# GpSimd in the order of the text from the first step on, a tile's ten gathers spread over the parts of a slot, each behind a ScalarE instruction

## The chip, the cores and the metric

The kernel runs on one core of one Trainium2 chip. The metric is device time in microseconds, the median of several runs. Profile times are microseconds from the start of the profiled execution's span. Engines: PE is TensorE's matmul part, PEld its weight loads, DVE VectorE, ACT ScalarE, POOL GpSimd, SP SyncE (which issues most DMAs, and shows as SPq). L889 is line 889 of the kernel before.

## The reference

A graph layer on N = 3327 nodes with D = 256 features. The input x is (3327, 256), adj is (3327, 3327), a sparse matrix with some 0.12% of its entries and the diagonal set.

```python
h = jnp.maximum(_layernorm(x), 0.0)
R = adj + I;  R = R / R.sum(-1, keepdims=True)
Z = 0;  Xf = h;  Xa = h
for n in range(2):
    A = _top_p_attention(Xa, W1, W2, W3)   # softmax of (Xa W1' W2')(Xa W3')',
    Xf = R @ Xf                            # cut to the top 0.9 of each row's mass, renormalised
    Xa = A @ Xa
    Z = Z + Xf @ U1[n].T + Xa @ U2[n].T
out = x + layernorm(h + Z) * ln_g + ln_b
```

## The kernel before

`guess_graph_layer` (L344) holds the run. The nodes are cut into NT = 26 tiles of 128 rows. Each of the two steps is a loop of slots, `for i in range(-1, NT + 2)`. In slot i tile i's softmax row (128 x 3328) gets its threshold and is scaled (VectorE L726, L731 to L764, L760; `settle`), the logits of tile i + 1 are made (TensorE L598, ScalarE L602 to L608; `measured`), and tile i − 1's row is turned by TensorE in blocks of four (L806), copied by ScalarE (L808) and summed with the nodes (L820; `Sums`). Queries and keys of later tiles come from L521 to L543 (`project`): a TensorE product L521, ScalarE copies L526 and L530, VectorE L536, and five small GpSimd instructions L539 to L543; GpSimd's L641 to L644 are four more small ones, for ScalarE's L652.

The sparse product R @ Xf is done by gathers. `listed` loads the adjacency of a tile in pieces of 256 KB (L841, tag `at`, two buffers, issued by SyncE), reduces each on VectorE (L842), and finds which 128-column blocks of each row hold an entry. The first four block numbers of a row go to `index[:, t, :4]` (GpSimd L851); the rest is packed by TensorE and ScalarE (`packed`, then L874 to L878) and VectorE's L881 into a fifth (GpSimd L882). With these a tile has ten gathers, indirect DMAs that GpSimd issues: five 128 x 128 pieces of the adjacency into `ac` (L889), five of node rows into `xg` (L898, 257 wide, from the table `bx`). A sixth block of `ac`, the diagonal one, comes by SyncE (L884) and gets the identity added by GpSimd (L886). Both tags have two buffers. Two slots later `spread` (L1075 on) multiplies them on TensorE (`diffuse`, L906), stores `ac` for the second step (`cx`, L1084, 384 KB, by SyncE, which waits until all six blocks are there), and writes the result on VectorE (L1087, L1088). `products` makes the tables `ax` and `bx` from the nodes at the start (L987, L993 and the stores L994, L995), through buffers that also hold the exponentials of L602. `first_end` (L914 on) has GpSimd's L923.

The order of work is written by hand. A slot has 7 parts; `PLAN` (L1104), with `BEGIN` for the first slots, is a string of letters for each part, and each letter moves one generator to its next `yield`: m measured, d settle, s spread, w weights, q project, e first_end, a the lister, p packed, g gathers, b products. A generator that is not through at the end of the slot is run to its end. After the letters of a part come the turns (L806, L808) and sums (L820). At the end (L1191 on), the instructions of TensorE, ScalarE and VectorE are chained in the text's order from `begin` on; those of GpSimd only from `ordered[0]` on, which is the start of the second step. In the first step GpSimd's order, and SyncE's throughout, is left to the scheduler. Most slots of the first step have this order on GpSimd: one xg, four ac, one xg, L886, two xg, L923, L882, the fifth ac, the fifth xg, L539 to L543, L641 to L644. On SyncE a slot has 5 or 6 loads L841, with sx (L924), cx (L1084), L884, own (L1078), vx (L1090) and s1 between them.

Of the kernel before, what the change touches and what calls it, by code (L numbers as in the profile page):

```python
# [14 lines left out]
ALU = mybir.AluOpType  # L15
# [5 lines left out]
D = 256  # L21
DA = 64
NT = (N + P - 1) // P
# [312 lines left out]
DIRECT = 4  # L336
LIST = 16
KT = DIRECT + 2
IN_ORDER = mybir.DependencyInfo(mybir.DependencyClass.NoSync, mybir.DependencyReason.DATA)
NONE = NP - 1  # L340

# [2 lines left out]
def guess_graph_layer(ctx, tc, x, adj, w1t, w2t, w3t, u1t, u2t, ln_g, ln_b, out, flag):  # L344
# [15 lines left out]
    V, G, S, PE = nc.vector, nc.gpsimd, nc.scalar, nc.tensor  # L360

    rows_of = lambda t: min(P, N - t * P)
    valid = lambda t: 0 <= t < NT
# [22 lines left out]
    ident = const.tile([P, P], F32, tag="ident", name="ident")  # L386
# [24 lines left out]
    one = const.tile([P, 8], F32, tag="one", name="one")  # L411
# [28 lines left out]
    bx = dram.tile([P, NT, D + 1], F32, tag="bx", name="bx")  # L440
# [429 lines left out]
    def gathered(t):  # L870
        oh = ohs.pop(t)
        ls, n = lists[:, t, :], LIST - DIRECT
        po = ps_t.tile([P, 4, P], F32, tag="pt", name="po")
        PE.matmul(po[:, 0, : n + 1], oh, ls[:, DIRECT:], start=True, stop=True)  # L874
        lo = small.tile([P, n], F32, tag="lo", name="lo", bufs=2)
        S.copy(lo, po[:, 0, :n])
        nth = small.tile([P, 1], F32, tag="nth", name="nth")
        S.activation(nth, po[:, 0, n : n + 1], AF.Identity, scale=-1.0, bias=part)  # L878
        yield
        of = small.tile([P, LIST], F32, tag="of", name="of", bufs=2)  # L880
        V.scalar_tensor_tensor(of[:, :n], place[:, :n], nth, lo, ALU.is_equal, ALU.mult, accum_out=nth)  # L881
        G.tensor_scalar(index[:, t, DIRECT:], nth, -1.0, float(NONE), ALU.mult, ALU.add)  # L882
        ac = adjp.tile([P, KT, P], F32, tag="ac", name="ac", bufs=2)
        nc.sync.dma_start(ac[:, KT - 1, :], adj[t, :, t, :])  # L884
        acs[t] = ac
        G.tensor_tensor(ac[:, KT - 1, :], ac[:, KT - 1, :], ident, ALU.add)  # L886
        rows = adj.rearrange("t p j r -> (t p j) r")
        for k in range(KT - 1):
            G.indirect_dma_start(out=ac[:, k, :], out_offset=None, in_=rows,  # L889
                                 in_offset=bass.IndirectOffsetOnAxis(ap=index[:, t, k : k + 1], axis=0),  # L890
                                 element_offset=t * P * NT * P)
        run(fetched(bx, t, D + 1))

    def fetched(table, t, w):
        xgs[t] = xg = adjp.tile([P, KT - 1, D + 1], F32, tag="xg", name="xg", bufs=2)
        rows = table.rearrange("p j d -> (p j) d")
        for k in range(KT - 1):
            G.indirect_dma_start(out=xg[:, k, :w], out_offset=None, in_=rows,  # L898
                                 in_offset=bass.IndirectOffsetOnAxis(ap=index[:, t, k : k + 1], axis=0))
            yield  # L900
# [59 lines left out]
    none = iter(())  # L960

    def run(work, n=99):
        for _ in range(n):
            next(work, None)
# [40 lines left out]
    for q in range(HALF + 5):  # L1005
        if 0 <= q - 3 < HALF:
            k, pk = q - 3, made.pop(q - 3)
# [86 lines left out]
    def refetch(t):  # L1094
        acs[t] = adjp.tile([P, KT, P], F32, tag="ac", name="ac", bufs=2)
        nc.sync.dma_start(acs[t].rearrange("p k r -> p (k r)"), cx[t])
        yield from fetched(vx, t, D)
# [3 lines left out]

    PLAN = (("mdsssa", "mcdsssa", "edawwp", "msda", "mpdea", "gdawwq", "emgq"),  # L1104
            ("llcmss", "lnms", "lwwnfd", "lcmdsssggggg", "fsmwqdf", "llmdf", "lmwd"))

    LAST = {NT - 1: ("cfss", "cn", "nd", "sss", "fdddddsf", "f", ""), NT: ("c", "", "", "ff", "ff", "fv", "f"),
            NT + 1: ("fv", "f", "", "", "f", "f", "f")}
    BEGIN = {-1: ("mba", "mmbba", "mwwbbaa", "bmwwb", "", "", ""),
             0: ("mdbba", "mcdbba", "medbwwbap", "mdabb", "mpdbwwba", "gdabbq", "q"),  # L1110
             1: ("mdsssbba", "mcdsssbba", "edbawwbp", "msdbga", "mpdea", "dawwq", "emgq")}
    OPEN = {-1: ("llcmss", "lnms", "lwwnfd", "lcmdsssggggg", "fmgswqdf", "llmdf", "lmwfdm"),
            0: ("cmssggg", "nms", "wwnfd", "cmdsss", "fsmgwqdf", "mdf", "mwd"),
            1: ("cmss", "nms", "wwnfd", "cmdsssggggg", "fsmwqdf", "mgdf", "mwd")}
    OPEN[2] = OPEN[3] = OPEN[1]
    fetching = itertools.chain(*(refetch(t) for t in range(NT)))
    LATE = (1, 4)
    BLOCKS = ({}, {1: (0, 1), 2: ()})
# [3 lines left out]
    ordered = []  # L1122
    for step in range(2):
        sums = Sums(step, live, xw if step else x0, AHEAD[step])

        for i in range(-1, NT + 2):
            if step == 0 and i == NT - 3:
                begun = [weights(1, t, live, False) for t in range(3)]
            if step == 1 and i == -1:
                ordered.append(len(trace))  # L1130
            if step == 1 and i == -1:
                run(begun[0])
                prove(0)
                for e in es[4:]:
                    G.memset(e[:, N:NP], 0.0)
            work.update(
                n=work["m"],
                c=work["d"],
                d=settle(step, i, live[step, i]) if valid(i) else none,
                m=measured(step, live[step, i + 1]) if valid(i + 1) else none,  # L1140
                s=spread(step, i - 2 + 2 * step) if valid(i - 2 + 2 * step) else none,
                w=later.pop((step, i + 2), none),
                e=first_end(i - 2) if step == 0 and valid(i - 2) else none,
                a=itertools.islice(lister, 5 + i % 2 if i > 0 else 6) if step == 0 else none,
                p=packed(i + 1) if step == 0 and i >= 0 and valid(i + 1) else none,
                g=fetching if step else itertools.chain(work.get("g", none), gathered(i)) if valid(i) else none,
                b=none if step else product, q=none, v=proof() if step and i == NT else work.get("v", none),
                l=laws(range(3, NT)) if step and i == -1 else work["l"] if step and i == 0 else none,
            )
            if i >= 0 and valid(i + 3):  # L1150
                later[step, i + 3] = weights(step, i + 3, live)
                work["q"] = itertools.islice(later[step, i + 3], 2 - step)
            if step == 0 and i >= NT - 2 and i < NT + 1:

                work["w"] = itertools.islice(begun[i - NT + 2], CUT - 1)
            if step == 0 and i >= NT - 3 and i < NT:
                work["q"] = itertools.islice(begun[i - NT + 3], 1)
            if i == -1:
                work["w"] = begun[1] if step == 0 else itertools.chain(begun[1], begun[2])
            if step == 0 and i == 0:  # L1160
                work["w"] = begun[2]
            for k in range(PARTS):
                g = PARTS * (i - 1) + k - LATE[step]
                summing = valid(g // PARTS)
                if step and valid((g + AHEAD[1]) // PARTS):
                    sums.turn(g + (k == 2), min(i, NT - 1))
                for c in ({**OPEN, **LAST} if step else BEGIN).get(i, PLAN[step])[k]:
                    next(work[c], None)
                if summing and not step:
                    sums.turn(g, min(i, NT - 1))  # L1170
                for n in BLOCKS[step].get(k, (0,)) if summing else ():
                    ended = sums.sum(g + n)
                    if ended and step == 0:
                        live["r", ended[0]] = ended[1]
                    elif ended:
                        work["f"] = finish(ended[0], live.pop(("f", ended[0])), *ended[1])
            if step == 1 and i == -1:
                run(work["m"])
            if step == 0 and i == -1:
                G.memset(es[2][:, N:NP], 0.0)  # L1180
            if step and i < 1:
                next(fetching)
            for c in ("lcnwqsepb" if i > -1 else "cnwqsepb") if step else "cmwqsep" + "gb" * (i > 0):
                run(work[c])
            if step == 0 and i == NT:
                moments(1, gsum)
                for t in range(3):
                    live[1, t]["ms"] = returned(project(1, t, queries=False))
    run(work["f"])

    for engine, since in ((PE.engine, begin), (S.engine, begin), (V.engine, begin), (G.engine, ordered[0])):  # L1191
        queue = [i for i in trace[since:] if i.engine == engine]
        for one_, next_ in zip(queue, queue[1:]):
            tc.add_manual_dep(next_, one_.name, IN_ORDER, reason="order of the text")

# [43 lines left out]
```

## Time and profile before

| what | value |
|---|---|
| median of 3 runs | 1396.95 us (1394.01 to 1402.68) |
| profiled execution | 1402.92 us, span 1401.2 us, clock 0.98 |
| busy: PE, PEld | 1276.6 us (91%), 976.5 us (70%) |
| busy: DVE, ACT, POOL | 1199.8 us (86%), 1102.5 us (79%), 814.9 us (58%) |
| gathers from in_adj, L889 | 130, 142.8 us busy, 1099 ns each |
| gathers from bx, L898 | 130, 165.0 us busy, 1269 ns each |
| SyncE at L1084 waiting for ac | 112.1 us, 25 times |
| first step, by the stretches used | start to 130 us, 130 to 710 us |

The page has a busy time for each engine and, in its fifth part, groups of instructions by line: busy time, mean duration, then the idle time just ahead of them on their engine and what ended it. The waits list, for each line, what ended a wait, the total, how often and the longest. The timeline gives single instructions: start, duration, engine, line, output and inputs, and in brackets the idle time before it with what ended it. For a gather, the duration on POOL is the work of issuing it.

### The profile page before, as it was taken

What the parts mean: (1) busy time and instruction counts of PE and PEld (TensorE: products, weight loads), DVE (VectorE), ACT (ScalarE), POOL (GpSimd) and SP (SyncE); (2) the same over time, 40 slices, a digit from 0 to 9 for tenths busy, and PEclk for the clock granted to TensorE, in tenths of its full rate; (3) what the DMA queues carried; (4) which work ended last, traced back from release to release, by engine and by line L of the source; (5) the groups of instructions that cost most, each with busy time, mean ns of one, the idle gap of its engine ahead of it and who ended that gap; (6) DMA issues with size and microseconds to landing.
All of it is one profiled execution on the core that took longest, in us unless ns stands there. A gap on an engine that the chain in (4) does not pass through costs nothing.

```text
span 1401.2 us, 22108 instructions
## 1 busy us (share of the span) xinstructions
PE 1276.6 (91%) x6495; PEld 976.5 (70%) x6495; DVE 1199.8 (86%) x3689; ACT 1102.5 (79%) x2445; POOL 814.9 (58%) x1244
## 2 busy tenths in 40 slices
PE   5898899999999999999999769999999999999985
PEld 4535777777777777677677547777777777777764
DVE  6878788989999899889882589999998999999984
ACT  5566686778887788778764689999999999999941
POOL 6213888766777667566573475655645556555522
PEclk9999999999999999999999879999999999999998
DMA  8754454453444545444432221221322213122200
GB/s 290 242 167 141 126 153 132 124 148 111 140 142 127 140 117 151 124 126 134 114 82 79 62 63 53 79 84 53 91 61 75 79 58 91 57 79 80 57 20 22
DMA packets 92642, 149.77 MB, mean 107 GB/s; under 512 B 15425, under 2 KB 59072, under 8 KB 92512
## 3 DMA queue, kind: packets, MB, share of 16 engines
q1 hardware_dynamic: 75056, 105.37, 23.9%
q0 software_dynamic: 16640, 42.69, 12.3%
q8 instruction: 54, 0.88, 0.3%
q14 instruction: 76, 0.62, 0.1%
q10 hardware_dynamic: 816, 0.20, 0.1%
HBM read 120.93 MB, written 27.28 MB: 106 GB/s over the span
## 4 chain that ended last, share of the span: by engine, by line
DVE 43%; PE 41%; ACT 9%; issue 5%; POOL 1%; DMA 1%; SPq 0%; DVEq 0%; POOLq 0%; ACTq 0%
PE pa L820 17%; DVE cand L731 9%; DVE w L726 8%; PE pt L806 5%; DVE e L760 5%; PE pl L598 4%; PE pr L906 4%; DVE cand L740 4%; DVE bb L738 3%; PE pz L919 3%; ACT ja L631 3%; DVE x L760 2%; PE pz L987 2%; ACT eT L808 1%; DVE fm L842 1%
## 5 line engine op out<-in xcount | busy, mean ns | idle before, releaser
L820 PE MATMUL pa<-xw,eT 128*128 128x256 f32 x1352 | 324.8, 385 | 27.4 <-DVE s L930 26.2
L631 ACT ACTIVATE ja<-e,g 128x3328 uint8<-128x3328 f32 x106 | 325.8, 3073 | 0.1
L820 PE MATMUL pa<-x,eT 128*128 128x256 f32 x1352 | 324.1, 381 | 0.0
L820 PEld LDWEIGHTS pa<-xw,eT 128*128 128x128 f32 x1352 | 251.6, 191 | 78.2 <-DVE s L930 31.6
L808 ACT COPY eT<-pt 128x512 f32<-128x512 f32 (+1 forms) x364 | 200.7, 559 | 106.5 <-PE pt L806 76.1
L820 PEld LDWEIGHTS pa<-x,eT 128*128 128x128 f32 x1352 | 244.3, 191 | 26.1
L731 DVE MAX8 cand<-w 128x8 f32<-128x168 f32 (+1 forms) x1040 | 251.4, 317 | 0.0
L898 POOL DMA_INDIRECT xg<-bx,index x130 | 165.0, 1269 | 52.0 <-issue 41.6
L806 PE MATMUL pt<-ident,e 128*128 128x128 f32 x1144 | 176.5, 277 | 15.2 <-DVE e L757 9.1
L806 PEld LDWEIGHTS pt<-ident,e 128*128 128x128 f32 x1144 | 141.0, 144 | 55.2 <-issue 27.9
L889 POOL DMA_INDIRECT ac<-in_adj,index x130 | 142.8, 1099 | 43.9 <-issue 29.1
L726 DVE SCALAR_TENSOR_TENSOR w<-e,g 128x3328 f32<-128x3328 f32 x44 | 162.1, 3684 | 0.7
L898 POOL DMA_INDIRECT xg<-vx,index x130 | 129.5, 996 | 38.6 <-issue 38.6
L906 PE MATMUL pr<-xg,ac 128*128 128x257 f32 (+1 forms) x520 | 141.9, 397 | 9.9 <-DVE s L1088 6.3
L760 DVE SCALAR_TENSOR_TENSOR e<-e,rec 128x3328 f32<-128x3328 f32 x40 | 147.7, 3691 | 0.6
L602 ACT ACTIVATE e<-pl 128x832 f32<-128x832 f32 x132 | 113.7, 866 | 16.4 <-PE pl L598 12.0
L906 PEld LDWEIGHTS pr<-xg,ac 128*128 128x128 f32 x520 | 94.2, 195 | 36.4 <-issue 14.6
L738 DVE MAX8 bb<-cand 128x8 f32<-128x160 f32 x286 | 92.6, 324 | 6.7 <-DVE cand L740 0.3
L598 PE MATMUL pl<-both,qT 64*128 64x416 f32 x416 | 91.7, 542 | 6.5 <-DVE e L993 3.5
L598 PE MATMUL pl<-after,qT 64*128 64x416 f32 x416 | 95.9, 555 | 0.0
L842 DVE TENSOR_REDUCE fm<-at 128x4 f32<-128x512 f32 (+1 forms) x133 | 84.5, 635 | 12.8 <-DMA at<-in_adj 11.8
L674 POOL TENSOR_SCALAR g<-g,law 128x1 f32<-128x1 f32 x23 | 46.4, 2016 | 67.1 <-ACT g L673 67.1
(258 smaller groups left out, 2087.3 us busy)
## 6 DMA issues: line engine op xcount, KB each, us to landing
at<-in_adj SPq DMA_DIRECT2D x114, 256.0 KB
cx<-ac SPq DMA_DIRECT2D x26, 384.0 KB
ac<-cx SPq DMA_DIRECT2D x26, 384.0 KB
wide<-in_adj SPq DMA_DIRECT2D x8, 832.0 KB
e<-in_adj SPq DMA_DIRECT2D x6, 832.0 KB
own<-bx SPq DMA_DIRECT2D x26, 128.5 KB
x<-in_x SPq DMA_DIRECT2D x13, 256.0 KB
s<-ax SPq DMA_DIRECT2D x26, 128.0 KB
```

The costliest lines, as they stand in the source:

```text
L598: PE.matmul(pl[:, a, :wd], qT[p, :], keys_of(step, a).rearrange("p a b -> p (a b)")[:, c : c + wd], start=True, stop=True)
L631: S.activation(ja, e, f, bias=guess, scale=sign, accum_out=total)
L726: V.scalar_tensor_tensor(w, e, col(16), e, ALU.is_lt, ALU.mult, accum_out=d2)
L731: V.max(cand[:, 8 * s : 8 * s + 8], w[:, s * SEG : min(NP, (s + 1) * SEG)])
L738: V.max(b8, cand)
L760: V.scalar_tensor_tensor(e, e, at(1), e, ALU.is_ge, ALU.mult, accum_out=ra)
L806: PE.transpose(pt[:, j, :], e[:, (j0 + j) * P : (j0 + j + 1) * P], ident)
L808: S.copy(eT[:, :w, :], pt[:, :w, :])
L820: PE.matmul(self.pa, eT[:, c - 4 * k, :], self.xa[:, j, :], start=c == 0, stop=c == NT - 1)
L889: G.indirect_dma_start(out=ac[:, k, :], out_offset=None, in_=rows, in_offset=bass.IndirectOffsetOnAxis(ap=index[:, t, k : k + 1], axis=0), ...
L898: G.indirect_dma_start(out=xg[:, k, :w], out_offset=None, in_=rows, in_offset=bass.IndirectOffsetOnAxis(ap=index[:, t, k : k + 1], axis=0))
L906: PE.matmul(pr[:, :w], ac[:, k, :], own if k == KT - 1 else xg[:, k, :w], start=k == 0, stop=k == KT - 1)
```

## The change

GpSimd is chained in the text's order from `begin` on. `gathered` is split in two. Its first half (new letter h) makes the fifth block number. The gathers are a chain of their own, `spacing`, in which each letter g issues one. `spaced` gives the order for a tile: ac 0 to 3, xg 0 to 3, the fifth ac with the identity addition, the fifth xg; for tiles 0 and 1 together: five ac of tile 0, four of tile 1, five xg of tile 0, the fifth ac of tile 1, five xg of tile 1. `PLAN` has ten g in a slot, one or two in a part. The first GpSimd instruction of each g gets a dependence (`BEHIND`) on the last ScalarE instruction that stands ahead of it in the text. (The fifth pair of a tile is issued at the start of the slot after.) The diff, cut to its core:

```diff
--- before.py
+++ after.py
@@ -336,6 +336,7 @@
 DIRECT = 4
 LIST = 16
 KT = DIRECT + 2
+BEHIND = mybir.DependencyInfo(mybir.DependencyClass.Sync, mybir.DependencyReason.DATA)
 IN_ORDER = mybir.DependencyInfo(mybir.DependencyClass.NoSync, mybir.DependencyReason.DATA)
 NONE = NP - 1
 
@@ -880,16 +881,27 @@
         of = small.tile([P, LIST], F32, tag="of", name="of", bufs=2)
         V.scalar_tensor_tensor(of[:, :n], place[:, :n], nth, lo, ALU.is_equal, ALU.mult, accum_out=nth)
         G.tensor_scalar(index[:, t, DIRECT:], nth, -1.0, float(NONE), ALU.mult, ALU.add)
+
+    def adjacent(t):
         ac = adjp.tile([P, KT, P], F32, tag="ac", name="ac", bufs=2)
         nc.sync.dma_start(ac[:, KT - 1, :], adj[t, :, t, :])
         acs[t] = ac
-        G.tensor_tensor(ac[:, KT - 1, :], ac[:, KT - 1, :], ident, ALU.add)
         rows = adj.rearrange("t p j r -> (t p j) r")
         for k in range(KT - 1):
             G.indirect_dma_start(out=ac[:, k, :], out_offset=None, in_=rows,
                                  in_offset=bass.IndirectOffsetOnAxis(ap=index[:, t, k : k + 1], axis=0),
                                  element_offset=t * P * NT * P)
-        run(fetched(bx, t, D + 1))
+            if k == KT - 2:
+                G.tensor_tensor(ac[:, KT - 1, :], ac[:, KT - 1, :], ident, ALU.add)
+            yield
+
+    def spaced(few):
+
+        both_ = [(adjacent(t), fetched(bx, t, D + 1)) for t in few]
+        if len(few) > 1:
+            (a, f), (b, h) = both_
+            return itertools.chain(a, itertools.islice(b, DIRECT), f, b, h)
+        return itertools.chain(*(itertools.islice(a, n) for n in (DIRECT, 1) for a in both_[0]))
 
     def fetched(table, t, w):
         xgs[t] = xg = adjp.tile([P, KT - 1, D + 1], F32, tag="xg", name="xg", bufs=2)
@@ -1101,18 +1113,20 @@
 
 
 
-    PLAN = (("mdsssa", "mcdsssa", "edawwp", "msda", "mpdea", "gdawwq", "emgq"),
+    PLAN = (("gmdsssa", "gmcdsssa", "edawwpg", "gmsdga", "gmpdea", "hgdawwqg", "gehmgq"),
             ("llcmss", "lnms", "lwwnfd", "lcmdsssggggg", "fsmwqdf", "llmdf", "lmwd"))
 
     LAST = {NT - 1: ("cfss", "cn", "nd", "sss", "fdddddsf", "f", ""), NT: ("c", "", "", "ff", "ff", "fv", "f"),
             NT + 1: ("fv", "f", "", "", "f", "f", "f")}
     BEGIN = {-1: ("mba", "mmbba", "mwwbbaa", "bmwwb", "", "", ""),
-             0: ("mdbba", "mcdbba", "medbwwbap", "mdabb", "mpdbwwba", "gdabbq", "q"),
-             1: ("mdsssbba", "mcdsssbba", "edbawwbp", "msdbga", "mpdea", "dawwq", "emgq")}
+             0: ("mdbba", "mcdbba", "medbwwbap", "mdabb", "gmpdbwwba", "hgdabgbq", "hgq"),
+             1: ("ggmdsssbba", "gmcdgsssbba", "gedbawwbp", "msdbga", "gmpdeag", "hgdawwqg", "hgemgq"),
+             2: ("gmdsssa", "gmcdsssga", "gedawwpg", "gmsdga", "gmpdea", "hgdawwqg", "gehmgq")}
     OPEN = {-1: ("llcmss", "lnms", "lwwnfd", "lcmdsssggggg", "fmgswqdf", "llmdf", "lmwfdm"),
             0: ("cmssggg", "nms", "wwnfd", "cmdsss", "fsmgwqdf", "mdf", "mwd"),
             1: ("cmss", "nms", "wwnfd", "cmdsssggggg", "fsmwqdf", "mgdf", "mwd")}
     OPEN[2] = OPEN[3] = OPEN[1]
+    spacing = itertools.chain(spaced((0, 1)), *(spaced((t,)) for t in range(2, NT)))
     fetching = itertools.chain(*(refetch(t) for t in range(NT)))
     LATE = (1, 4)
     BLOCKS = ({}, {1: (0, 1), 2: ()})
@@ -1143,7 +1157,8 @@
                 e=first_end(i - 2) if step == 0 and valid(i - 2) else none,
                 a=itertools.islice(lister, 5 + i % 2 if i > 0 else 6) if step == 0 else none,
                 p=packed(i + 1) if step == 0 and i >= 0 and valid(i + 1) else none,
-                g=fetching if step else itertools.chain(work.get("g", none), gathered(i)) if valid(i) else none,
+                g=fetching if step else spacing if i > -1 else none,
+                h=gathered(i) if step == 0 and valid(i) else none,
                 b=none if step else product, q=none, v=proof() if step and i == NT else work.get("v", none),
                 l=laws(range(3, NT)) if step and i == -1 else work["l"] if step and i == 0 else none,
             )
@@ -1165,7 +1180,12 @@
                 if step and valid((g + AHEAD[1]) // PARTS):
                     sums.turn(g + (k == 2), min(i, NT - 1))
                 for c in ({**OPEN, **LAST} if step else BEGIN).get(i, PLAN[step])[k]:
+                    at = len(trace)
                     next(work[c], None)
+                    if c == "g" and not step and len(trace) > at:
+                        gate = next(n for n in reversed(trace[:at]) if n.engine == S.engine)
+                        issue = next(n for n in trace[at:] if n.engine == G.engine)
+                        tc.add_manual_dep(issue, gate.name, BEHIND, reason="one by one")
                 if summing and not step:
                     sums.turn(g, min(i, NT - 1))
                 for n in BLOCKS[step].get(k, (0,)) if summing else ():
@@ -1180,7 +1200,7 @@
                 G.memset(es[2][:, N:NP], 0.0)
             if step and i < 1:
                 next(fetching)
-            for c in ("lcnwqsepb" if i > -1 else "cnwqsepb") if step else "cmwqsep" + "gb" * (i > 0):
+            for c in ("lcnwqsepb" if i > -1 else "cnwqsepb") if step else "cmwqseph" + "b" * (i > 0):
                 run(work[c])
             if step == 0 and i == NT:
                 moments(1, gsum)
@@ -1188,7 +1208,7 @@
                     live[1, t]["ms"] = returned(project(1, t, queries=False))
     run(work["f"])
 
-    for engine, since in ((PE.engine, begin), (S.engine, begin), (V.engine, begin), (G.engine, ordered[0])):
+    for engine, since in ((PE.engine, begin), (S.engine, begin), (V.engine, begin), (G.engine, begin)):
         queue = [i for i in trace[since:] if i.engine == engine]
         for one_, next_ in zip(queue, queue[1:]):
             tc.add_manual_dep(next_, one_.name, IN_ORDER, reason="order of the text")
```

With it each engine has as many instructions as before. TensorE's order differs in one place: the L874 of tile 1 comes two turns later. ScalarE's L876 and L878 of that tile follow it. On VectorE, L881 of each tile stands ahead of L660 to L664 rather than behind. GpSimd's order in most slots becomes: the fifth ac of the tile before, L886, L641 to L644, the fifth xg of the tile before, four ac, L923, three xg, L882, one xg, L539 to L543. SyncE's order, which the scheduler makes, has each cx one L841 later than before (sx, at, cx, at becomes sx, at, at, cx; sx, cx, at, at becomes sx, at, cx, at), and the cx of tile 0 stands ahead of the eight stores ax and bx of tiles 18 to 21, where it stood behind them and those of tiles 22 and 23.

## The prediction

> **What bounds the kernel now.** I read the busy time by stretch first, because the change touches the first step alone. A row of this view gives the stretch, its length, then busy time and instruction count of PE, PE's loads, DVE, ACT and POOL, the granted clock, the DMA share and GB/s:
>
> ```profile
> 300.00:400.00 100.00, 96.85 (x514) 75.81 (x514) 92.05 (x286) 81.69 (x204) 70.41 (x92) 1.00 0.45 130
> ```
>
> TensorE does 96.85 of 100 us, VectorE 92.05. A slot (the period from one L726 to the next, 166.91 to 676.47 us over 20 slots) takes 25.48 us. POOL's 70.41 bound nothing by themselves. Next the waits, TensorE's over 130 to 740 us, then VectorE's over 200 to 690:
>
> ```profile
> PE pq L521 <- ACT eT L808: 24.4, 19, 1.9
> PE pr L906 <- DMA xg<-bx,index: 3.6, 2, 3.0
> ```
>
> ```profile
> DVE mq L536 <- issue: 13.5, 7, 1.9
> DVE mq L536 <- ACT mq L530: 9.0, 7, 1.6
> DVE of L881 <- ACT nth L878: 3.3, 5, 0.8
> DVE fm L842 <- DMA at<-in_adj: 2.4, 3, 1.0
> ```
>
> TensorE's only steady gap, 1.3 us a slot, comes from ScalarE. Gathers stop it twice, 3.6 us in all, at the start. VectorE's slack is the first three rows, 25.8 us over some 19 slots: 1.4 us a slot, all ahead of L726. Against it stands what the lister's loads (L841) cost, 2.4 us here and 11.8 us in the whole run.
>
> Last, what the tenth gather holds back. POOL and then SyncE around one L726, which runs from 447.16 to 450.84:
>
> ```profile
> 445.87 0.99 POOL L889 DMA_INDIRECT ac<-in_adj,index  x1 [0.51 <-POOL index L882]
> 447.17 0.95 POOL L898 DMA_INDIRECT xg<-bx,index  x1 [0.30 <-issue]
> 448.14 3.13 POOL L539 TENSOR_TENSOR ms<-ms,half 128x1 f32<-128x1 f32 x1
> ```
>
> ```profile
> 445.35 0.37 SPq L841 DMA_DIRECT2D at<-in_adj  x1
> 449.16 0.33 SPq L1084 DMA_DIRECT2D cx<-ac  x1
> 451.72 0.33 SPq L841 DMA_DIRECT2D at<-in_adj  x1
> ```
>
> The tile's last adjacency gather ends at 446.86. The store of ac (cx, L1084) is issued 2.3 us later, L726 +2.0, and the next load 2.6 us after it. SyncE waits 112.1 us in all, 25 times, for ac at L1084: everything queued behind waits too. The third POOL row is the second thing to see: an operation that lasts 0.59 us elsewhere runs exactly to the end of L726 plus 0.4. An L889 gather at 396.85, inside an L726 that began at 396.12, took 3.82 us instead of 0.95.
>
> [...] the transfer follows. Here it lands about 1.9 to 2.3 us later, by the cx issues.
>
> **The change, part by part.** It adds no instruction; TensorE, ScalarE and VectorE keep their order but for tile 0's and 1's L874 to L881 and for L881, which moves ahead of L660 to L664 (1.3 us of work with slack): 0. POOL gets the text's order from the start, each gather waits for a ScalarE instruction, and SyncE's cx falls behind one more load.
>
> *Start.* Today POOL idles 27.70 us before L539 at 107.52. In the new order ac0 to ac3 of tile 0 stand ahead of it, ac3 behind L530 (ends 107.17). Issue follows at about 107.4, inside the L726 of 107.35 to 111.04; it ends at 111.04 + 0.87 = 111.9 (0.87 from 396.85 + 3.82 against L726's end at 399.80). L539 to L543 (1.7 us by their rows at 425.26) reach 113.9, ac4 is issued at 114.2, ends at 115.2, and lands near 117.3. cx of tile 0 stands ahead of eight stores of ax and bx in the new SyncE order; today it is behind them:
>
> ```profile
> 111.92 0.32 SPq L994 DMA_DIRECT2D ax<-e  x1
> ...
> 115.24 0.44 SPq L995 DMA_DIRECT2D bx<-e  x1
> ```
>
> They take 3.8 us, so run 117.6 to 121.5 instead of 111.92 to 115.68. ScalarE's row 118.25 (L602, after 2.10 us idle for the buffer these stores read; a load is named, but the last bx store was issued 3.0 us before and the tile L602 writes is its source) then starts at about 124.1: +5.9. TensorE's pz at 120.95 waits on the same chain with 0.7 to spare: **+5.1 us**. Bounds: [...] 6 if nothing is absorbed.
>
> *Each later slot, 3 to 20 (where loads are listed).* Measured from L726: xg1 is gated by L530, which ends 0.2 us before L726 begins. If it falls inside L726, it ends at +4.58; then xg2 (1.25), L882, xg3, L539 to L543 (1.7) and ac4 end at about +10.5, so cx goes at +12.6 instead of today's +1.7 to +2.7. A load behind cx lands late: at 175.86 cx was issued, the load behind it at 176.29, and VectorE had it 3.1 us later, after a 2.35 us stall:
>
> ```profile
> 175.86 0.33 SPq L1084 DMA_DIRECT2D cx<-ac  x1
> 176.29 1.05 SPq L841 DMA_DIRECT2D at<-in_adj  x2
> ```
>
> ```profile
> 179.43 0.69 DVE L842 TENSOR_REDUCE fm<-at 128x4 f32<-128x512 f32 x1 [2.35 <-DMA at<-in_adj]
> ```
>
> So the load is there at 12.6 + 0.4 + 3.1 = +16.1 to +16.7; L842 asks at +13.5 to +14.7. The stall is 2.5 us (mean of 1.4 and 3.2, rounded up for the later load). But a stalled VectorE comes later to its next L726, and then xg1 slips through ahead of it. With L726 over 0.45 us behind L530 the chain is 1.2 us shorter, the stall about 1.3; with more than 1.6, 0.2. The 1.4 us of slack is spent exactly on this, so I expect the lag to settle near 1 us with a stall of 1.3. L760 then ends 2 to 3 us later; the transposes that need it start at 447.71 today against its end at 443.03, 4.7 us (3.3 in the tightest slot). Hidden, then, with 0 to 0.2 us left over: 18 × 0.1 = **+2 us**. Without that cover each slot costs 2.5 − 1.4 = 1.1 us, +20. Bounds 0 and 18 × 1.8 = 32 (a stall of 3.2 every time). What is late next: cx, and behind it the loads and vx, s1 and own on SyncE; readers of cx come a whole step later.
>
> *Rest.* The order after the first step is unchanged: 0. L641 to L644, moved to about +8.5, are needed by L652 at +16.7: 0.
>
> Sum +7 us on the profiled span of 1401.2 (its execution: 1402.92): about 1408. The median of the runs is 1396.95, so **about 1404**.
>
> **Rivals.** *A, the forecast*: VectorE's slack takes the stalls, 1404, itself 1398 to 1411. *B, slower*: the load wait becomes the bound: POOL meets L726 in every slot. For: L530 ends 0.2 us before L726 today, and VectorE's 92% leaves little. Against: a stall itself moves L726 away. It decides once the stall exceeds 1.4 us a slot: 18 × 1.1 + 5 = +25, **1422**. *C, faster*: gathers spread out reach their users in time and leave loads alone; it takes back at most the 3.6 us TensorE waits for xg and VectorE's 11.8 us for loads, −15.4, **1381**. For: both waits lie in the first third, where gathers bunch. Against: cx, not the bunching, delays loads, and it gets later. *D, nothing happens*: gates are met whenever a gather's turn comes and the start is hidden, **1397**.
>
> **Chances.** A 0.45, B 0.35, C 0.12, D 0.08. This kernel's measurement tells about 1% from no change. Faster than 1383: C, and a little less than all of it, 0.11. Slower than 1411: B, with some of A's tail, 0.38. Within: 0.51. The range starts above C (1390) and ends at 1425, just over B: it leaves out C and the part of B toward its bound (1434), near 0.2.
>
> **What would show it.** Right: cx issued at L726 +10 to +13 in most slots of the first step; "DVE fm L842 <- DMA at" rising from 11.8 to some 30 us while "DVE mq L536" waits shrink toward 0; ScalarE's first late L602 near 124; 25.5 to 25.6 us a slot. B shows in a slot above 26.3 us with TensorE waiting for VectorE at L806. Wrong at the root: cx still near +2, or gathers that never meet L726. The start is wrong if the eight stores stay near 112. It would be wrong in sign if TensorE's 1.3 us gap at L521 shrank.

## The result and the profile after

The kernel after has a median of 1413.87 us (1410.48 to 1414.44, 4 runs), the kernel before, in the runs beside it, 1396.36 us (1394.01 to 1402.68, 4 runs). The ratio is 1.0115 [1.0098, 1.0133]: 17.5 us slower, where 7 were forecast. The profiled execution of after took 1413.57 us (span 1411.6 us, clock 0.971), that of before 1402.92 us. The two profiles thus differ by 10.4 us of span only; the runs of before spread over 9 us, and the profiled one is 6.5 us above their median.

In the code of after, lines have moved: L726 is L727, L760 L761, L806 L807, L808 L809, L820 L821, L521 L522, L536 L537, L602 L603, L841 L842, L842 L843, L889 L891, L898 L910, L994 and L995 L1006 and L1007, L1084 L1096.

Where the time went, in the profiles: before the first changed instruction the executions already differ by 3.0 us (the first L726 at 75.0, L727 at 78.0; other executions lie anywhere between), which is no effect of the change. Slots 0 to 3 add 3.4 us, slots 3 to 23 add 7.0 (25.82 us each, 25.47 before), the last three tiles give 2.8 back, the second step nothing. First the stretch shown of before, now of after, with the same columns:

```profile
300.00:400.00 100.00, 95.17 (x500) 75.18 (x499) 86.89 (x272) 79.23 (x195) 76.97 (x92) 0.98 0.45 132
```

VectorE fell from 92.05 to 86.89 us of 100, TensorE only from 96.85 to 95.17, and its clock is no longer 1.00. The waits tell why. TensorE's over 130 to 740 us, its first two rows and the one that stood first before, then VectorE's over 200 to 690, first row:

```profile
PE pt L807 <- DVE e L761: 28.4, 15, 4.1
PE pr L918 <- DMA xg<-bx,index: 3.2, 1, 3.2
...
PE pq L522 <- ACT eT L809: 0.3, 1, 0.3
```

```profile
DVE fm L843 <- DMA at<-in_adj: 32.8, 13, 5.4
```

Two things happened, and only one was forecast. VectorE waits for the lister's loads (47.5 us in the whole run, 11.8 before), its waits ahead of L537 are gone, and TensorE waits for VectorE at L807. And TensorE's gap at L521, 24.4 us before, which the forecast left as it was, has vanished.

One slot, whose L727 runs from 434.63 to 438.31 and whose L761 started at 429.85, on POOL and SyncE, and the load's reader on VectorE:

```profile
431.01 3.33 POOL L910 DMA_INDIRECT xg<-bx,index  x1 [0.30 <-issue]
...
434.89 4.27 POOL L910 DMA_INDIRECT xg<-bx,index  x1 [0.27 <-issue]
...
441.62 1.11 POOL L891 DMA_INDIRECT ac<-in_adj,index  x1 [0.17 <-issue]
```

```profile
439.19 0.33 SPq L842 DMA_DIRECT2D at<-in_adj  x1
445.12 0.33 SPq L1096 DMA_DIRECT2D cx<-ac  x1
445.54 0.38 SPq L842 DMA_DIRECT2D at<-in_adj  x1
```

```profile
450.54 0.69 DVE L843 TENSOR_REDUCE fm<-at 128x4 f32<-128x512 f32 x1 [2.30 <-DMA at<-in_adj]
```

Two gathers take 3.33 and 4.27 us instead of 0.95, each until some 0.8 us after the end of one of VectorE's instructions of 3.7 us: the second is the one that the forecast put inside L727, the first is caught in L761, which was not thought of. Not every gather is caught: the one of before at 447.17, 0.01 us after the start of L726, took 0.95 us. What holds the two long ones was not shown. The fifth adjacency gather goes at 441.62, cx 3.5 us later, L727 + 10.5, and for the 5.9 us between the first two SyncE rows no load is issued. The load behind cx then reaches VectorE 5.4 us after cx was issued.

### The profile page after: what moved, and what is told of

The parts are those of the page before. It is cut to its first block, busy times and chain, and to the rows that moved or that the text cites. A ratio compares the mean times of both kernels' runs of the same rounds, so it can differ in the third digit from the quotient of the medians.

```text
span 1411.6 us, 22249 instructions
## 1 busy us (share of the span) xinstructions
PE 1282.7 (91%) x6495; PEld 987.6 (70%) x6495; DVE 1199.3 (85%) x3689; ACT 1105.4 (78%) x2445; POOL 848.9 (60%) x1244
## 4 chain that ended last, share of the span: by engine, by line
DVE 64%; PE 15%; ACT 8%; DMA 7%; issue 4%; POOL 1%; SPq 1%; DVEq 0%; POOLq 0%; ACTq 0%
DVE cand L732 13%; DVE w L727 11%; DVE e L761 10%; DMA at<-in_adj 5%; PE pa L821 5%; DVE fm L843 5%; DVE bb L739 4%; DVE cand L741 4%; ACT ja L632 4%; PE pz L999 2%; PE pl L599 2%; DVE x L761 2%; PE pt L807 1%; PE pr L918 1%; DVE s L1100 1%
## 5 line engine op out<-in xcount | busy, mean ns | idle before, releaser
L821 PE MATMUL pa<-xw,eT 128*128 128x256 f32 x1352 | 324.4, 385 | 27.3 <-DVE s L942 26.1
L821 PE MATMUL pa<-x,eT 128*128 128x256 f32 x1352 | 328.1, 385 | 0.0
L821 PEld LDWEIGHTS pa<-xw,eT 128*128 128x128 f32 x1352 | 251.3, 191 | 77.9 <-DVE s L942 31.5
L821 PEld LDWEIGHTS pa<-x,eT 128*128 128x128 f32 x1352 | 246.8, 193 | 27.0
L910 POOL DMA_INDIRECT xg<-bx,index x130 | 213.9, 1645 | 81.5 <-ACT nth L879 27.2
L809 ACT COPY eT<-pt 128x512 f32<-128x512 f32 (+1 forms) x364 | 200.1, 557 | 78.4 <-PE pt L807 76.3
L807 PE MATMUL pt<-ident,e 128*128 128x128 f32 x1144 | 177.4, 278 | 41.3 <-DVE e L761 30.8
L807 PEld LDWEIGHTS pt<-ident,e 128*128 128x128 f32 x1144 | 140.9, 144 | 83.0 <-issue 53.5
L891 POOL DMA_INDIRECT ac<-in_adj,index x130 | 132.2, 1017 | 72.8 <-issue 24.7
L727 DVE SCALAR_TENSOR_TENSOR w<-e,g 128x3328 f32<-128x3328 f32 x44 | 162.2, 3688 | 0.7
L910 POOL DMA_INDIRECT xg<-vx,index x130 | 129.4, 995 | 38.6 <-issue 38.6
L761 DVE SCALAR_TENSOR_TENSOR e<-e,rec 128x3328 f32<-128x3328 f32 x40 | 148.6, 3715 | 0.6
L603 ACT ACTIVATE e<-pl 128x832 f32<-128x832 f32 x132 | 113.1, 861 | 33.7 <-PE pl L599 23.5
L843 DVE TENSOR_REDUCE fm<-at 128x4 f32<-128x512 f32 (+1 forms) x133 | 84.6, 636 | 53.9 <-DMA at<-in_adj 47.5
```

The source lines that it names most:

```text
L727: V.scalar_tensor_tensor(w, e, col(16), e, ALU.is_lt, ALU.mult, accum_out=d2)
L761: V.scalar_tensor_tensor(e, e, at(1), e, ALU.is_ge, ALU.mult, accum_out=ra)
L807: PE.transpose(pt[:, j, :], e[:, (j0 + j) * P : (j0 + j + 1) * P], ident)
L809: S.copy(eT[:, :w, :], pt[:, :w, :])
L821: PE.matmul(self.pa, eT[:, c - 4 * k, :], self.xa[:, j, :], start=c == 0, stop=c == NT - 1)
L843: V.tensor_reduce(fm[:, j0 : j0 + n], at[:, :n], AX.X, ALU.max, apply_absolute_value=True)
```

## The experiments

The runs were made on six chips, here P to U; kernels on one chip share the runs of before on it. "Place" is after with each cx kept in its place of the text on SyncE. "Slot us" is the mean period of L726 (L727) over slots 3 to 23, from the profiled execution.

| run | kernel | chip | median us | before there | ratio [95%] | slot us |
|---|---|---|---|---|---|---|
| e1_cx_place | place | P | 1365.25 | 1404.66 | 0.9726 [0.9704, 0.9749] | 23.78 |
| e2_cx_first | place, tile 0 only | P | 1405.18 | 1404.66 | 1.0013 [0.9998, 1.0029] | 26.09 |
| e3_no_gate | after, no waits on ScalarE | P | 1433.1 | 1404.66 | 1.019 [1.0163, 1.0217] | 27.21 |
| e4_same | before | P | 1403.68 | 1404.66 | 0.9995 [0.9983, 1.0007] | 25.80 |
| e5_after | after | Q | 1412.63 | 1395.71 | 1.011 [1.0087, 1.0133] | 25.89 |
| e6_place_nogate | place, no waits on ScalarE | Q | 1364.82 | 1395.71 | 0.9774 [0.975, 0.9798] | 23.82 |
| e7_place_run8 | place, eight gathers in a run | Q | 1382.47 | 1395.71 | 0.9885 [0.9859, 0.991] | 24.92 |
| e8_before_pause | before, a pause in its run of eight | Q | 1389.45 | 1395.71 | 0.9943 [0.9923, 0.9962] | 24.83 |
| e9_before_place | before, cx in place | R | 1367.98 | 1374.85 | 0.9951 [0.9935, 0.9968] | 23.99 |
| e10_cx_first_again | as e2 | R | 1407.14 | 1374.85 | 1.0235 [1.0209, 1.0261] | 25.90 |
| e11_after_again | after | R | 1413.9 | 1374.85 | 1.0281 [1.0262, 1.03] | 25.80 |
| e12_ac4_early | after, fifth ac ahead of the fourth xg | R | 1384.81 | 1374.85 | 1.007 [1.0052, 1.0087] | 24.72 |
| e13_same_again | before | S | 1394.24 | 1395.29 | 0.9992 [0.9979, 1.0004] | 25.25 |
| e14_place_again | place | S | 1365.14 | 1395.29 | 0.9788 [0.9775, 0.9802] | 23.78 |
| e15_run8_again | as e7 | S | 1383.95 | 1395.29 | 0.9915 [0.9902, 0.9929] | 24.88 |
| e16_same_third | before | T | 1404.35 | 1403.26 | 1.0004 [0.9992, 1.0017] | 25.39 |
| e17_run8_third | as e7 | T | 1388.32 | 1403.26 | 0.9876 [0.984, 0.9911] | 25.10 |
| e18_before_place_again | before, cx in place | U | 1367.67 | 1376.0 | 0.9934 [0.9911, 0.9956] | 24.03 |

One column must be read first: after takes 1412 to 1414 us and place 1365 (with or without the waits on ScalarE) on each of the three chips where they ran, but before takes 1375, 1396 or 1404 by the chip. A ratio to before mixes the two, so kernels are compared within a chip where they can be.

### Is it the store in SyncE's queue?

The theory after the first result was that the loads and the start's stores queue behind a cx that waits. In e1 each cx is tied behind the SyncE instruction that stands ahead of it in the text; the loads can then no longer fall behind it. In e2 the same, for tile 0 alone.

```diff
         if step == 0:
-            nc.sync.dma_start(cx[t], a.rearrange("p k r -> p (k r)"))
+            ahead = next(n for n in reversed(trace) if n.engine == nc.sync.engine)
+            store = nc.sync.dma_start(cx[t], a.rearrange("p k r -> p (k r)"))
+            if True:
+                tc.add_manual_dep(trace[-1], ahead.name, IN_ORDER, reason="not ahead of its place")
```

(e2 has `if t == 0:`.)

> The changed kernel, with each store cx kept behind the SyncE instruction that stands last ahead of it in the text, so that it no longer stops the queue while the tile's fifth ac gather is outstanding. Theory Q (SyncE's queue: loads and the ax and bx stores stand behind a cx that waits for a late gather): VectorE's wait for loads falls from 47.5 us to under 12, TensorE's waits for L761 from 30.8 us to under 5, ScalarE's 6.63 us idle near 120 us goes; the time is 1395 to 1400. Rival G (the gathers themselves come late for TensorE[...]): nothing of this store matters, 1411 to 1416.

> As the run before, but for the store of tile 0 alone: the eight ax and bx stores stand ahead of it again. Theory Q: the start's part alone comes back, 3.3 us by the profiles (slot 3 begins 6.4 us later, of which 3.0 stood before the first gather), up to 5.1 us as predicted: 1408 to 1411. The waits of the later slots stay. Rival G: 1413 to 1415.

e1 takes 1365.25 us, far below both kernels. Its cx goes even later, at L727 + 14.5 to + 20.3, but little waits for it: SyncE sits at it 44.7 us in 5 waits (after: 173.3 in 27), and over the slots 3 to 23 VectorE no longer waits for loads at all (after: 35.7 us). What costs is a load behind a waiting store, not a late store. TensorE over the slots 3 to 23, by stretch, of before, of after and of e1:

```profile
166.90:676.40 509.50, 483.73 (x2539) 376.05 (x2539) 459.41 (x1421) 403.66 (x1000) 358.85 (x471) 1.00 0.46 132
```

```profile
173.30:689.80 516.50, 488.15 (x2558) 385.61 (x2557) 458.09 (x1421) 406.31 (x1004) 391.40 (x467) 0.98 0.46 129
```

```profile
164.90:640.50 475.60, 475.60 (x2542) 377.62 (x2541) 456.12 (x1421) 405.05 (x1001) 386.69 (x464) 1.00 0.49 140
```

The same twenty slots take 509.50, 516.50 and 475.60 us, and in e1 TensorE is never idle. After against e1 is 28.35 us idle plus 12.55 us more busy, 40.9 in all, 2.0 a slot. The busy part goes with the clock: after's longest wait at L807 and what follows it on PE,

```profile
226.68 1.09 PE L807 MATMUL pt<-ident,e 128*128 128x128 f32 x4 [4.11 <-DVE e L761]
227.56 3.62 PE L821 MATMUL pa<-x,eT 128*128 128x256 f32 x8
```

are two groups that take 0.60 and 1.89 us otherwise. The granted clock from 225 to 237.5 us is 0.73. In after's stretch it falls to 0.50 four times, for 17.1 us in all (in e1 never). Half of that, 8.5 us, is an estimate of what the clock makes of the 12.55 us; the rest is open.

e2 gives back only the start. On P after did not run, so e10 and e11 measure the start's size side by side on one chip:

> The changed kernel with the store of tile 0 alone in its place, beside the changed kernel on one chip, since the two ratios stood on different chips. From the profiles (slot 3 begins 4.6 to 6.2 us earlier, the later slots as long): 4 to 7 us less than the changed kernel beside it. If the difference of the ratios was real: 13 us less.

> The changed kernel, the other side of that comparison: 1.008 to 1.013 of the kernel before.

e11 less e10 is 6.8 us: the start. On chip Q the whole effect of the queue is e5 less e6, 47.8 us (e6 also lacks the waits on ScalarE, which will be seen to be worth nothing there). The 6.8 of the start and 2.0 for each of 20 slots make 46.8 of it.

> The changed kernel, unchanged, on the chip of the runs beside it: 1.010 to 1.014 times the kernel before. By this ratio the store of tile 0 alone (the earlier run at 1.0013) is worth 10 us and more, where the profiles show 3.3 to 6.8 us at slot 3; a second profile shows whether the steady slots differ from execution to execution.

> Each cx in its place, and no waits on ScalarE: only the order of the gathers is left of the change. Theory H (TensorE's completion signals are held back while a long run of gathers is under way, and come about 1.3 us after its last one; the order of the text cuts the run of seven or eight to runs of five): still without the holds, 1365 to 1380, 0.972 to 0.983 of the kernel before. Rival W (the waits on ScalarE are what frees TensorE): 1395 and more.

Is the delay of the fifth ac gather what puts cx late? e12 issues it one gather sooner, ahead of the fourth xg and so of L540 to L544, nothing else:

```diff
-        return itertools.chain(*(itertools.islice(a, n) for n in (DIRECT, 1) for a in both_[0]))
+        (a, f), = both_
+        return itertools.chain(itertools.islice(a, DIRECT), itertools.islice(f, DIRECT - 1), a, f)
```

> The changed kernel with a tile's fifth ac gather (and the identity addition) ahead of its fourth and fifth xg gather, from tile 2 on; the store stays where it is in SyncE's queue. Theory Q: the gather comes out behind L727 but ahead of L540 to L544, so cx goes at about L727 +6.5 instead of +10 to +13, the load behind it is there by +10.5, before VectorE asks at +13.5: waits for loads under 15 us instead of 41 to 47, slots near 24 us, 1372 to 1385 with the late start still in it. If not the time of cx but its mere place ahead of a load decides, nothing changes: 1.01.

cx goes at L727 + 7.1 to + 9.6 instead of + 10.1 to + 13.0, the load waits of the whole run are 29.5 us instead of 55.9, and the kernel takes 29.1 us less than after, both on the same chip (e11). So the cost is graded: 3 us of delay are worth some 1.1 us a slot.

### The waits on ScalarE

e3 leaves the dependence out, of after; e6, above, leaves it out of place.

```diff
-                    if c == "g" and not step and len(trace) > at:
+                    if False:
                         gate = next(n for n in reversed(trace[:at]) if n.engine == S.engine)
```

> The changed kernel without the waits on ScalarE; GpSimd's order is the same. Theory Q: xg0 to xg2 follow ac3 at once and are out before L761 and L727, so the fifth ac gather waits only for L540 to L544, which follow VectorE's L537: cx at about L727 +6 to +8 instead of +10 to +13, half of the steady loss gone and the start better too: 1400 to 1406. Rival H (the order alone is the loss, the waits on ScalarE are met anyway): 1412 to 1415.

e3 missed its expectation by 27 us: 1433.1. The cx still goes late (L727 + 8.7 to + 13.2), the load waits grow to 76.2 us, up to 8.5 at a time, and TensorE waits at another place too (27.3 us at L931 for L1100's result). With cx in place the waits are worth nothing: 1364.82 without (e6), 1365.25 and 1365.14 with (e1, e14). With cx late they save some 20 us against after's 1412 to 1414, though after and e3 did not run on one chip. Why a gather that goes sooner makes late loads worse was not separated.

### Where did the gap at L521 go?

Place against before is −39.4 us on P, −30.9 on Q and −30.2 on S. The change must therefore hold a gain that the late stores hide. Before was profiled again, in e4:

> The kernel before, unchanged, for a second profile: 1394 to 1399. Its profiled execution shows where one execution of it differs from another: I expect the 6.6 us by which the first profile stood above the median in the stretch between the steps (700 to 800 us), where that profile is 6 us longer than the changed kernel's, and the first 75 us within 3 us.

ScalarE, TensorE and POOL around one gap of e4 (the lines are before's):

```profile
618.06 3.10 ACT L631 ACTIVATE ja<-e,g 128x3328 uint8<-128x3328 f32 x1
...
624.54 0.58 ACT L808 COPY eT<-pt 128x512 f32<-128x512 f32 x1 [3.29 <-PE pt L806]
```

```profile
618.88 0.60 PE L806 MATMUL pt<-ident,e 128*128 128x128 f32 x4
...
628.55 0.49 PE L521 MATMUL pq<-both,w2d 64*128 64x128 f32 x2 [1.38 <-ACT eT L808]
```

```profile
622.23 0.95 POOL L898 DMA_INDIRECT xg<-bx,index  x1 [0.30 <-issue]
```

The transposes that the copy needs end at 619.48, yet ScalarE, free at 621.25, starts the copy at 624.54, 5.1 us after them. What ended just before is the last of a run of eight gathers that began at 612.96: 623.18, 1.4 us before the copy. The trace also holds the times at which TensorE's semaphore was updated, the one that ScalarE's copies wait for and so TensorE's signal to them; no view prints them. Usually an update comes 0.01 to 0.03 us after the end shown of its matmul. Here the updates for the matmuls that end at 619.48, 622.92 and 623.36 come together, between 624.52 and 624.71. The signal itself is late, not ScalarE.

Such late bursts, with no signalling matmul ending in the 0.3 us before, can be counted between 165 and 700 us. The four profiles of before (the first, e4, e13, e16) have 25 to 28 each, of which 17 to 20 come after the seventh or eighth gather of a run, 1.0 to 2.3 us after it. After, e1, e2, e3, e5, e6 and e14, whose runs there are rarely longer than five, have 3 to 7. The five traces of R and U (e9 to e12, e18) have none, in either step.

In this slot of e4 the update that the copy waited for came 5.0 us after the shown end of its matmul (619.48 to 624.52). What passes between the two was not shown.

If the long run is the cause, it must bring the gap back into place, and a pause in before must remove it. e7 puts eight g of place into one part; e8 makes xg 1 to 3 of tiles 2 to 22 of before wait for a later ScalarE instruction, the second L631 pass of the tile after (both cut to the lines that matter; e7 also has the lines of e1, and e8 those that collect `sixth` and `passes`):

```diff
-    PLAN = (("gmdsssa", "gmcdsssa", "edawwpg", "gmsdga", "gmpdea", "hgdawwqg", "gehmgq"),
+    PLAN = (("gmdsssa", "gmcdsssa", "edawwpgggggggg", "msda", "mpdea", "hdawwq", "ehmq"),
```

```diff
+    for t, k in itertools.product(range(2, NT - 3), range(1, DIRECT)):
+        tc.add_manual_dep(sixth[t, k], passes[2 * (t + 1) + 1].name, BEHIND, reason="a pause")
```

> Each cx in its place, and in the slots from 2 on ac0 to ac3 and xg0 to xg3 of a tile follow one another in one part, a run of eight (the fifth pair stays in the first two parts). Theory H: the holds are back in each slot, TensorE's gaps at L522 too, slots of 25.3 to 26 us instead of 23.8: 1395 to 1410, 0.995 to 1.005 of the kernel before. Rival W or any theory by which the store alone counts: 1365 to 1372.

> The kernel before with one addition: for tiles 2 to 22, the second, third and fourth xg gather wait for ScalarE's second pass (L634) of the slot in which they run, about 2 us, which cuts the run of eight to five and three. Theory H: the signal for the next L808 copy comes on time, the 1.3 us gap at L521 goes, and with the short cx wait of the kernel before the slots fall to 24 us: 1365 to 1380. Rival (the run has nothing to do with the gap): 1396 to 1406, as the kernel before.

Both moved the right way and by less than expected. e7 is 17.7 us slower than e6 on its chip, with 19 late bursts (e15 21, e17 23), and TensorE waits again, though at L807 and not at L522. Its first row over 165 to 700 us:

```profile
PE pt L807 <- ACT nth L879: 13.8, 14, 3.1
```

e8 is 6.3 us faster than before; TensorE's gap at L521 falls to 9.1 us, but VectorE waits 13.7 us for loads. Its pause cut the run to five and three in 13 slots and left nine runs of eight, and 28 late bursts remain. So it moved them more than it removed them, and runs of five are not safe by themselves. Repeats of e7 and place beside before:

> The kernel before again, for a profile on another chip, if one is given. Where the runs beside it take about 1375 (as on the chip of the last four), theory H says that TensorE's signals come on time there: no waits of 1.3 us at L521 slot after slot (under 5 us in all, 26.1 in the last profile of this kernel), slots of 24 to 24.5 us. Where they take 1395 to 1405 again, the gaps are there again. If a profile of 1375 shows the gaps, or one of 1400 does not, H is wrong.

> The changed kernel with each cx in its place, on the same chip: 1364 to 1367 whatever the chip, since neither holds nor late stores are left. Against a kernel before of 1375 that is 0.993, against one of 1396 to 1405 it is 0.973 to 0.978.

> The run of eight with cx in its place, on the same chip: 1380 to 1385 again where the kernel before takes 1395 to 1405; where it takes 1375, theory H says the run costs nothing: 1364 to 1370. If it costs 18 us there too, the run costs by something else than held signals.

> As the run of this kernel before it: where it takes about 1375, no gaps of 1.3 us at L521 slot after slot and slots of 24 to 24.5 us (theory H); where it takes 1390 or more, the gaps. A third possibility, a time between the two, should go with gaps in some of the slots.

> As the run of this kernel before it: 1364 to 1370 where the kernel before takes about 1375, 1380 to 1386 where it takes 1390 or more.

They agree: e15 is 18.8 us above e14. The L521 gap of before over 165 to 700 us is 18.6 us in e13 on S, and 21.0 in e16 on T and 23.9 in e4 on P, where before is slower.

The last question was what the two parts are worth alone. e9 and e18 keep before's gathers, in their run of eight, and put cx in its place with the lines of e1:

> The kernel before, with each cx kept in its place behind the SyncE instruction that stands last ahead of it in the text; the rest is unchanged. It completes a square with the kernel before, the changed kernel and the changed kernel with cx in its place (0.973, 0.977). Theory: the order of the gathers is worth its 2.5% only where the store is out of the way, and the store's place alone is worth little where its gather is early (waits for loads 9.5 us in all): the long runs and the gaps at L521 stay, 0.990 to 1.001 of the kernel before. Rival (the place of the store is the whole gain of those two kernels): 0.973 to 0.980.

> The kernel before with each cx in its place, which took 1368 where the kernel before took 1375. On a chip where the kernel before takes 1390 or more, theory H: the runs of eight and the gaps at L521 (over 15 us) are there, 0.99 to 1.00 of the kernel before, some 20 us above the other chip. If it takes 1365 to 1370 there too, with no gaps, the place of the store removed the late signals, and they are no property of the chip and the run of gathers alone.

They ran on the chips where before itself takes 1375 and 1376, and in their traces the signals are not late. In e9, around the same instructions:

```profile
515.08 3.10 ACT L631 ACTIVATE ja<-e,g 128x3328 uint8<-128x3328 f32 x1
...
518.14 0.60 ACT L808 COPY eT<-pt 128x512 f32<-128x512 f32 x1
```

```profile
515.90 0.60 PE L806 MATMUL pt<-ident,e 128*128 128x128 f32 x4
```

The copy starts the moment ScalarE is free, in the middle of the same eight gathers (513.31 to 523.54). TensorE then has no steady gap (its waits over 165 to 700 us are 0.6 us). It is the chip and not the place of cx: e10, e11 and e12 on R have cx late and no late signal either, while e7 on Q has cx in place and 19 late bursts. Before itself takes 20 to 30 us less on R and U than on the others; its own profile wasn't taken there. There cx in place is worth 6.9 and 8.3 us, and the new order of the gathers no more than the 3 us between 1368 and place's 1365 on the other chips. On P, Q and S the two together are worth 30 to 39 us; taking 7 to 8 for the store, which was not measured there, leaves 22 to 32 for the order of the gathers.

Place, 1365 us on three chips (P and S with the waits on ScalarE, Q without), is the best version.

## Why the prediction was wrong in size

**The account.** The change holds a loss of about 48 us (loads and stores behind a late cx) and, on the chips where TensorE's signals come late, a gain of about 31 (before to place, on Q and S). On Q the two leave the 16.9 us between before and after. On R, where no signal comes late, nearly the whole loss shows: after is 39.1 us slower than before (e11). The forecast had 7 us of the one and nothing of the other; that it came near was partly the two cancelling.

**Start, +5.1.** Right in its mechanism, and near in size. cx of tile 0 goes ahead of the eight stores, and ScalarE's L603 waits for them:

```profile
119.37 0.32 SPq L1096 DMA_DIRECT2D cx<-ac  x1
119.78 0.39 SPq L1006 DMA_DIRECT2D ax<-e  x1
```

```profile
125.80 0.86 ACT L603 ACTIVATE e<-pl 128x832 f32<-128x832 f32 x1 [6.63 <-DMA bx<-e]
```

With the 3.0 us that this execution was late from the outset, 119.37 is 116.4 on the clock of before (117.3 forecast) and 125.80 is 122.8 (124.1). In e10, slot 3 begins 5.1 us earlier than in e11, with the first L727 at 74.8 in both. The medians of the two differ by 6.8 us, over the bound of 6.

**cx and the load behind it.** The mechanism was right: cx at L727 + 10.1 to + 13.0, forecast + 12.6; the waits ahead of L537 gone. ("Today's +1.7 to +2.7" holds for 13 of the 20 slots of before, with + 1.6 as the least; six are at + 6.5 to + 7.1 and one at + 9.0.) The load was mis-sized: it comes 5.2 us after cx's issue as the mean of 17 stalled loads, where 0.4 + 3.1 were taken from a single slot of before. So the load waits are 47.5 us, not some 30.

**"Hidden, then, with 0 to 0.2 us left over: 18 × 0.1 = +2 us".** This is the step that failed. Where +2 was forecast, TensorE lost 40.9 us against e1 over the slots 3 to 23, 28.35 idle and 12.55 in longer busy time. The cover, the time between L760's end and the transposes, was taken from one slot of before, 4.7 us, "3.3 in the tightest". Over slots 3 to 22 of that trace it is 3.8 us in the mean and 1.1 in the tightest. And both the cover and the slack of 1.4 us a slot ahead of L536 hung on the late signals: a TensorE held up at L521 reaches L806 later, and VectorE's slack was waiting for ScalarE's L530 behind the same copies. In e9, which has before's gathers, cx in place and no late signals, the cover is 1.0 us in the mean, and over 200 to 690 us VectorE's whole slack at L536 is

```profile
DVE mq L536 <- ACT mq L530: 0.7, 1, 0.7
```

where before had 22.5. In e1, without the stalls, the cover is 3.0 us; in after it is used up, with the 15 waits of TensorE for L761 shown above. The change took away most of the late signals, and with them what was to hide the stalls. Even the bound of 32 was too low, since it counted stalls and not the lower clock after them.

**The gap at L521 as a constant.** The prediction named its shrinking as the sign that would prove it wrong, but named no cause by which it could. It was put down to ScalarE; ScalarE was itself waiting for transposes long done. The gap went from 24.4 to 0.3 us. The sign of the result stayed, because the loss was larger.

**From the profile to the median.** +7 was added to a profiled span that lay 6.5 us above before's median, and the sum carried over to 1404. The runs of after hardly spread, those of before do. The difference between the medians is 7 us larger than that between the profiles for this reason alone.

**Rivals.** B, the load wait as the bound, with TensorE waiting at L806, is what the slots show, at 25.82 us and not over 26.3, as the vanished gap paid for part. C, faster by gathers that come in time, is no part of it: the gain came from another place. D is excluded, gathers do meet L727.

**Left open.** What holds TensorE's signals back during a long run of gathers, and what is different on R and U. The traces of the other chips also lack records of the other engines' updates (e4's has 1408 for the 1732 of ScalarE; those of R and U are complete). So the counts of late bursts are rough, and it is open whether the recording of the profile has a part in them. The second step was not touched, though it too has 22 to 34 late bursts in every trace but those of R and U. Before with cx in place on a chip where they come late wasn't run. Nor is it settled why the waits on ScalarE matter when cx is late, or why TensorE is 8.1 us more busy in the slots of before than in e1's at almost the same clock.

## What to carry to other kernels

When a gather is moved later, look at who waits for it in a shared queue, and tie that waiter behind what must not wait for it; here two lines turned 1413 us into 1365. Before slack or cover is used to hide a stall, ask which wait made it and whether the change removes that wait: it may take the cover along. And where an engine waits for a result that the trace shows long done, suspect that the release itself is late, and look for what ended just before it. Compare versions on one chip.

## What was unexpected of the hardware

- TensorE's signals can come microseconds after the shown end of its matmul (5.0 us in the slot shown of e4) while GpSimd issues a long run of gathers. Between 165 and 700 us this happened 25 to 28 times in before, 19 to 23 times in place with runs of eight, 3 to 7 times where runs were mostly of five or fewer, but 28 times in e8, whose runs were cut in part. On R and U it never did, not even with the runs of eight of e9 and e18. That the gathers are the cause is inferred from e7 and from where the late updates stand; what links the two is not known.
- One and the same kernel takes 1375, 1396 or 1404 us by the chip, while two others stay within 2 us on the chips where they ran.
- TensorE's granted clock was 0.50 around the end of some short waits. With the wait of 4.11 us in after it was 0.50 for 6.83 us, and a group of 1.89 us took 3.62. Waits of 2.25, 2.44 and 2.46 us came with 3.41 us at 0.50 each, while five others in the slots 3 to 23, of 2.08 to 3.11 us, came with none. So the length of the wait alone does not decide it; what else does was not shown.
